# Where VectorE sums the last pair's products: ahead of the next pair's first product, or behind the plain second operand's products

## The chip, the cores and the metric

The kernel runs on one core of one Trainium2 chip. The metric is the device time of one launch in microseconds (us), taken as the median of several runs. The engines are named as in the profile: PE (TensorE, the matmuls), PEld (its weight loads), DVE (VectorE), ACT (ScalarE), POOL (GpSimd) and SP (SyncE, which only issues DMAs here). L526 is line 526 of the kernel.

## The reference

A "compressed interaction network" over `r_x` of 1024 samples, 64 fields and an embedding of 16, in float32. Cut to what matters:

```
x0 = h = x                                   # (1024, 64, 16)
for i in range(3):
    z = einsum('bfe,bge->bfge', x0, h)       # products of fields, per embedding place
    y = einsum('oc,bce->boe', W[i], z.reshape(B, 64*64, 16)) + b[i]
    x_i, h = (y[:, :64], y[:, 64:]) if i < 2 else (y, y)
    xs.append(x_i)
pooled = sum(concatenate(xs, axis=1), axis=2)   # over the embedding
return pooled @ fc_w.T + fc_b                # (1024, 1)
```

The last sum, over the 16 places of the embedding, is the one that the change moves.

## The kernel before, in words

**Tiling.** The samples are cut into 32 chunks of 32; a chunk has 32 x 16 = 512 columns. Two chunks make a pair, and there are 16 pairs. Three pairs are done in a prologue of their own form; the other thirteen (`pairs`, with `k` = 3 to 15) go through one scheme, one pair in a window of PE work.

**The work of a pair.** For each of its two chunks, called `a` and `b`, DVE multiplies field rows with rotated field rows, a block of 128 x 2048 at a time (`w_product`, recorded at L634, or `plain`/`product`, recorded at L242). A pair's blocks are named by their part in the scheme: `X` and `B21` from chunk `a`, `B22` and `T3` from chunk `b`, each with a half j = 0 and a half j = 1. `T3` is made from the sum of two operands (`w_both`, L640). POOL makes sums and differences of blocks (`w_mix`, L651; one of them is a DMA that adds, L649): `T2 = X - T3`, then `T3 = B22 + T2`, then `T2 = T2 + B21`. PE contracts the blocks with weights (`w_job`, through `mm`, L526) into the PSUM banks `alpha`, `delta` and `beta`. DVE reads those banks when a pair ends and forms products of 64 x 512 and 128 x 512 in the tile `uu` (`w_hb` L672, `w_qa` L676, `w_uu` L682, `w_ha` L679, `x_v0x` L290). Last, `sums` (L294) adds `uu` over the embedding into the pair's own columns of the tile `acc`, which nothing reads before the end of the kernel (`add_parts`, `pools`).

**PE's two columns.** The matmuls of a window come in two lists, `columns`, which `zipped` interleaves one by one; each uses its own half of PE's columns, so two run side by side. One list begins with the `X` products into `alpha`, the other with the `T3` products into `delta`. `X` goes in the order j = 1, then j = 0. So the first block that a window needs, as its very first step, is `X` with j = 1: the "first product" of this document. Which list comes first in the interleaving alternates from pair to pair. Near a window's end stand four short matmuls, `squares`, with 64 rows.

**The order of the work.** It is written out by hand. Every operation is put on a list with a planned time (`at(when, ...)`); the list is sorted by it, and the functions are called in that order, which fixes each engine's own queue. The planned times act through the order alone. Window n begins at `t = T0 + SPAN * n` with `SPAN = 31`. In it the pair `p` runs on PE, the pair before it, `q`, is ended on DVE, and the products of the next pair are made:

```
make_pair(
    t, p, (-21.4, -18.7, -18.4, -15.8, -12.2, -9.5, -6.1, -2, 1.6, 4.2),
    (-5, 1.6, 3.6, 7.2, 12.4, 18.6, 18.5),
)
quads = 30.2 if n == NPAIR - 1 else 22.9
window(t, p, (first_fill(q), second_fill(q)), late_run(q), quads=quads)
end_pair(t, q, (0.7, 11.7, 17.9, 22.3, 23.2, 18.4, 27.5))
```

The first list of `make_pair` are the times of `B22` j=0, `w_both`, `T3` j=0, `X` j=0, `B22` j=1, `w_both`, `T3` j=1, `X` j=1, `B21` j=0, `B21` j=1. The list of `end_pair` are the times of `w_hb`, `w_qa`, `w_uu`, `w_ha`, `w_uu`, `x_v0x` and `sums`, in the order of its parameters `hb_, qa, uub, ha, uua, xv, add`:

```
def end_pair(t, p, whens):
    hb_, qa, uub, ha, uua, xv, add = whens
    ...
    at(t + add, sums, p["k"])
```

A second operand is first copied into PSUM by ACT (`second`, L554), into one of two banks that rotate. Blocks come from a list of 14 (`take`, `used`). Loads are issued by SP: `xa` (L146), `xb` (L160), `e` (L164), `xx` (L169).

DVE's queue through one window, in the order before, is thus:

| place | operation | recorded at |
|---|---|---|
| 1 | `sums` of the pair before last | L294 |
| 2 | `X` j=1 of the next pair (first product) | L634 |
| 3 | `w_hb` of the pair that just ran | L672 |
| 4, 5 | `B21` j=0 and j=1 of the next pair (the plain second operand's products) | L634 |
| 6 | `B22` j=0 of the pair after it | L634 |
| 7 | `w_qa` | L676 |
| 8 to 10 | `w_both`, `T3` j=0, `X` j=0 | L640, L634 |
| 11, 12 | `w_uu` from `alpha`, `x_v0x` | L682, L290 |
| 13 to 16 | `B22` j=1, `w_both`, `w_ha`, `w_uu` from `delta` | L634, L640, L679, L682 |
| 17 | `T3` j=1; then place 1 again | L634 |

Of the kernel before, what the change touches and what calls it, by code (L numbers as in the profile page):

```python
# [70 lines left out]
def cin_kernel(ctx, tc, xra, xrb, wh, w0r, w1h, w2t, wx1, wx0, vec, out):  # L71
# [444 lines left out]
    def at(when, fn, *args, **flags):  # L516
        ops.append((when, len(ops), fn, args, flags))
# [168 lines left out]
    def make_pair(t, p, when, mixed):  # L686
        a, b = p["a"], p["b"]
        for when, c, j, name, uses in (
            (when[0], b, 2, "B22", 5), (when[1], b, 0, None, 0), (when[2], b, 0, "T3", 9),
            (when[3], a, 0, "X", 5), (when[4], b, 3, "B22", 5), (when[5], b, 1, None, 0),  # L690
            (when[6], b, 1, "T3", 9), (when[7], a, 1, "X", 13 if p["k"] > 3 else 5), (when[8], a, 2, "B21", 5),
            (when[9], a, 3, "B21", 5),
        ):
            if name is None:
                at(t + when, w_both, p, j)
                continue
            if name == "B21" and j == 2 and p["k"] == 3:
                at(t + when, w_product, p, c, j, name, uses, engine=nc.gpsimd)
                continue
            if name != "T3":  # L700
                ahead = 3.3 if p["k"] > 4 and name == "B22" and j == 2 else 2.7
                if p["k"] == 3 and name == "X" and j == 1:
                    ahead = 9.1
                at(t + when - ahead, second, c, j)
            at(t + when, w_product, p, c, j, name, uses)
        t2, t1, t4 = ("T2", "X", "T3"), ("T3", "B22", "T2"), ("T2", "T2", "B21")
        for when, j, names in zip(
            mixed, (0, 1, 1, 0, 1, 1, 0), (t2, (*t2, 0, 2), (*t2, 2), t1, t1, t4, t4)
        ):
            at(t + when, w_mix, p, j, *names)  # L710
        at(t + 29, lambda: used(p["B21"][1]))
# [4 lines left out]
    def first_fill(p):  # L716
        return [(lambda: q_extra(p["a"], va, p["beta"]),)] + p4_run(p)[-LATE : -LATE // 2]

    def second_fill(p):
        return p4_run(p)[-LATE // 2 :]  # L720

    def late_run(p, out=alpha, first=0, last=2 * NI):
        jobs = w_run(p, out, s4, "B22", out is gamma)[first:last]
        return jobs if last < 2 * NI else jobs + [(lambda: q_extra(p["b"], vb, p["alpha"]),)]
# [8 lines left out]
    def window(t, p, fill, late, pad=[], order=GROUPS[NI:] + GROUPS[:NI], quads=22.9):  # L733
        columns = (
            w_run(p, alpha, wq_all, "X", True, order=order) + fill[0] + w_run(p, alpha, s2, "T2")
            + fill[1] + w_run(p, alpha, s1, "T3"),
            w_run(p, delta, s3, "T3", True) + late + w_run(p, beta, wq_all, "B21", True, 2 * NI)
            + pad + p4_run(p)[:-LATE],
        )
        zipped(t, *columns[:: -1 if p["k"] % 2 else 1])  # L740
        at(t + quads, squares, p)
        at(t + 7.6, snap_p1, p)
        at(t + 7.8, snap_p7, p)
        at(t + 7.6 + len(fill[0]) + 8, snap_u2, p)

    def end_pair(t, p, whens):
        hb_, qa, uub, ha, uua, xv, add = whens
        at(t + hb_, w_hb, p)
        at(t + qa, w_qa, p)
        at(t + uub, w_uu, p, alpha, "A", snaps[2])  # L750
        at(t + ha, w_ha, p)
        at(t + uua, w_uu, p, delta, "O", snaps[0])
        at(t + xv, x_v0x, p["k"])
        at(t + add, sums, p["k"])


    def load_pair(t, p, b0, a0, b1, a1):
        a, b = p["a"], p["b"]
        at(t + b0, load_xa, b)
        at(t + b0, load_xb, b, 2, 0)  # L760
        at(t + a0, load_xa, a)
        at(t + a0, load_xb, a, 0)
        at(t + b1, load_xb, b, 3, 1)
        at(t + a1, load_xb, a, 1, 2, 3)
        for c in (b, a):
            at(t + 1, load_e, c)
            at(t + 14, square, c)
        at(t + 1.1, load_xx, p["k"])
# [65 lines left out]
    for n in range(NPAIR):  # L834
        k = n + 3
        s = k % 2
        p = {
            "k": k, "A": halves[s], "O": halves[1 - s], "b": 2 * k + s, "a": 2 * k + 1 - s,
        }
        pairs.append(p)  # L840
        t = T0 + SPAN * n
        if n == 0:
            load_pair(t, p, -39.9, -33.3, -33.15, -27)
            make_pair(
                t, p, (-23.4, -20.7, -20.4, -17.8, -17.2, -16.8, -16.6, -7, -13.5, 3),
                (-14, -6.9, -6.8, 7.2, 12.4, 17.6, 17.5),
            )
            left5 = [[(contract_half, 5, 3, i, n) for i in (2, 3)] for n in range(2)]
            window(
                t, p, ([left5[1][0], (q_extra, 4, va)], [left5[1][1]]),  # L850
                [left5[0][0], (q_extra, 5, va), None, None], [left5[0][1], None],
                GROUPS, 21.9,
            )
        else:
            q = pairs[-2]
            load_pair(t, p, -34, -28, -27.8, -27.7)
# [3 lines that stand above are left out]
            )  # L860
            quads = 30.2 if n == NPAIR - 1 else 22.9
            window(t, p, (first_fill(q), second_fill(q)), late_run(q), quads=quads)
            end_pair(t, q, (0.7, 11.7, 17.9, 22.3, 23.2, 18.4, 27.5))


    NP = NCH // 2
# [37 lines left out]
    t, q = T0 + SPAN * NPAIR, pairs[-1]  # L904
# [183 lines left out]
```

## Time and profile before

| | |
|---|---|
| median of 3 runs | 452.44 us (451.9 to 452.5) |
| profiled execution | 453.01 us, of which the span of the trace is 451.2 us |
| PE | busy 445.1 us, 99% of the span |
| DVE | busy 393.1 us, 87% |
| POOL | busy 364.4 us, 81% |
| ACT | busy 116.8 us, 26% |
| granted clock of PE | 1.00 |
| `sums` in its full form, 128 x 1024 to 128 x 64 | 13 times, 1.209 us each |

The span is the time from the first to the last instruction of the program; the device time has 1.8 us more around it. Busy time of PE is modelled, since matmuls overlap, so that a busy PE may still lose time between two starts. Where such losses lie is read from the starts in the timeline.

### The profile page before, as it was taken

The page shows a single profiled execution, that of the slowest core. Times are in us where ns is not written, and L with a number is a line of the kernel's source. Part 1 is how long each engine was busy: PE and PEld are TensorE (multiplying, and loading weights), DVE is VectorE, ACT ScalarE, POOL GpSimd, SP SyncE. Part 2 cuts the span into 40 slices and gives each one's busy share as a digit, 9 for nine tenths or more (in the row PEclk, how much of TensorE's full clock was granted, in tenths as well). Part 3 has the DMA queues.
Part 4 walks back from the last instruction along what each step waited for, and adds up shares of the span by engine and source line. Part 5 has one row for each costly group of instructions (what it writes and reads, how often), then busy time and mean ns, then how long its engine had stood idle before and what let it go on. Part 6 is the DMA issues. An engine that isn't in the chain of part 4 may idle for free.

```text
span 451.2 us, 6067 instructions
## 1 busy us (share of the span) xinstructions
PE 445.1 (99%) x2302; PEld 178.9 (40%) x2302; DVE 393.1 (87%) x284; ACT 116.8 (26%) x215; POOL 364.4 (81%) x125
## 2 busy tenths in 40 slices
PE   7999999999999999999999999999999999999997
PEld 4565343442334433343333433344333433344435
DVE  3996598998989998999999899999989999998734
ACT  2163241323312213231221313131131313114111
POOL 5413687999996979899797979979797997979900
PEclk9999999999999999999999999999999999999999
DMA  8996999395949386694958769493967949591500
GB/s 297 415 306 157 322 393 359 114 336 155 324 114 333 121 226 256 133 360 105 281 179 230 259 153 336 107 319 135 252 238 161 341 105 314 176 270 44 107 0 2
DMA packets 34484, 99.67 MB, mean 221 GB/s; under 512 B 6324, under 2 KB 6996, under 8 KB 27864
## 3 DMA queue, kind: packets, MB, share of 16 engines
q1 hardware_dynamic: 31800, 84.70, 52.5%
q0 software_dynamic: 1872, 13.63, 16.9%
q10 hardware_dynamic: 784, 0.95, 0.8%
q8 instruction: 18, 0.29, 0.3%
q14 instruction: 10, 0.08, 0.0%
HBM read 84.00 MB, written 1.64 MB: 190 GB/s over the span
## 4 chain that ended last, share of the span: by engine, by line
PE 96%; DMA 2%; POOL 1%; SPq 0%; issue 0%; DVE 0%; ACT 0%; POOLq 0%; ACTq 0%
PE alpha L526 45%; PE delta L526 20%; PE beta L526 10%; PE acc L526 6%; PE acc L252 6%; PE q L526 3%; PE acc L270 3%; DMA z<-in_w0r 2%; POOL z L651 1%; PE y L526 0%; PE pm L386 0%; PE pv L359 0%; SPq L146 0%; PE xp L221 0%; PE hx L526 0%
## 5 line engine op out<-in xcount | busy, mean ns | idle before, releaser
L651 POOL TENSOR_TENSOR z<-z,z 128x2048 f32<-128x2048 f32 (+1 forms) x78 | 299.6, 3874 | 29.2 <-PE alpha L526 29.1
L634 DVE TENSOR_TENSOR z<-xa,xp 128x2048 f32<-128x2048 f32 x103 | 231.7, 2279 | 2.6 <-issue 1.4
L526 PE MATMUL alpha<-z,ws 128*64 128x512 f32 x624 | 222.1, 593 | 0.0
L526 PEld LDWEIGHTS alpha<-z,ws 128*64 128x64 f32 x624 | 71.7, 137 | 86.3 <-issue 85.5
L526 PE MATMUL delta<-z,w_all 128*64 128x512 f32 x208 | 95.6, 593 | 0.7 <-POOL z L651 0.7
L554 ACT COPY xp<-xb 128x512 f32<-128x512 f32 x88 | 51.6, 588 | 169.5 <-DVE z L634 141.6
L526 PE MATMUL beta<-z,w_all 128*64 128x512 f32 x208 | 93.8, 595 | 0.0
L526 PE MATMUL alpha<-z,w_all 128*64 128x512 f32 x208 | 92.0, 595 | 0.0
L526 PE MATMUL delta<-z,ws 128*64 128x512 f32 x208 | 91.6, 593 | 0.0
L242 DVE TENSOR_TENSOR z<-xa,xp 128x2048 f32<-128x2048 f32 (+2 forms) x23 | 45.0, 2002 | 6.3 <-ACT xp L554 4.8
L242 POOL TENSOR_TENSOR z<-xa,xb 128x2048 f32<-128x2048 f32 x6 | 27.5, 4646 | 19.6 <-DMA xb<-in_xrb 19.6
L526 PEld LDWEIGHTS delta<-z,w_all 128*64 128x64 f32 x208 | 28.3, 137 | 32.9 <-issue 30.4
L526 PEld LDWEIGHTS alpha<-z,w_all 128*64 128x64 f32 x208 | 27.5, 137 | 29.9 <-issue 24.0
L526 PEld LDWEIGHTS delta<-z,ws 128*64 128x64 f32 x208 | 28.1, 137 | 23.7 <-issue 22.8
L526 PEld LDWEIGHTS beta<-z,w_all 128*64 128x64 f32 x208 | 26.9, 137 | 24.2 <-issue 23.0
L252 PE MATMUL acc<-z,w_all 128*64 128x256 f32 x256 | 29.1, 382 | 2.3 <-DVE z L242 2.0
L526 PE MATMUL acc<-z,w_all 128*64 128x512 f32 (+1 forms) x96 | 29.7, 594 | 0.0
L252 PEld LDWEIGHTS acc<-z,w_all 128*64 128x64 f32 x256 | 18.0, 137 | 14.6 <-DVE z L242 3.8
L665 ACT ACTIVATE snap<-alpha,vs 64x512 f32<-64x512 f32 x13 | 8.9, 684 | 54.8 <-PE alpha L526 54.8
L294 DVE TENSOR_REDUCE acc<-uu 128x64 f32<-128x1024 f32 (+2 forms) x19 | 19.6, 1036 | 0.2
L682 DVE SCALAR_TENSOR_TENSOR uu<-alpha,snap 64x512 f32<-64x512 f32 x13 | 9.0, 689 | 12.2 <-PE alpha L526 12.2
L662 ACT COPY snap<-alpha 64x512 f32<-64x512 f32 x13 | 7.6, 581 | 46.2 <-PE alpha L526 29.7
(117 smaller groups left out, 356.4 us busy)
## 6 DMA issues: line engine op xcount, KB each, us to landing
xa<-in_xra SPq DMA_DIRECT2D x32, 1024.0 KB, 8.5
xb<-in_xrb SPq DMA_DIRECT2D x128, 256.0 KB, 8.0
z<-z POOLq DMA_DIRECT2D x13, 1024.0 KB, 8.5
e<-in_xra SPq DMA_DIRECT2D x28, 128.0 KB, 7.3
xx<-in_xra SPq DMA_DIRECT2D x28, 128.0 KB, 2.5
z<-in_w2t SPq DMA_DIRECT2D x2, 1024.0 KB
z<-in_wx SPq DMA_DIRECT2D x2, 1024.0 KB, 10.0
z<-in_w1h SPq DMA_DIRECT2D x1, 1024.0 KB
```

The lines of the kernel that those rows point to most:

```text
L242: engine.tensor_tensor(blocks[zs[c, j]][:, at, :], xas[c][:, at, :], xbs[c][j].unsqueeze(1).to_broadcast([128, last - first, N]), ALU.mult,)
L252: nc.tensor.matmul(accs[c][halves[n]], w_all[:, t, 0:64], blocks[zs[c, j]][:, i, n * H2 : (n + 1) * H2], start=(t == 0), stop=(j == last a ...
L270: nc.tensor.matmul(accs[c][halves[1 - c % 2]], w_all[:, t, 64:128], blocks[zs[c, j]][:, i, :], start=(t == 0), stop=False, skip_group_chec ...
L294: nc.vector.tensor_reduce(acc[rows, of, k, half], uu[rows, of if at is None else at, E * half.start : E * half.stop].rearrange("p k (b e) ...
L526: nc.tensor.matmul(out, w, rhs, start=start, stop=stop, skip_group_check=True)
L554: nc.scalar.copy(bank, xbs[c][j])
L634: engine.tensor_tensor(blocks[b], xas[c], xbs[c][j].unsqueeze(1).to_broadcast([128, NI, N]), ALU.mult)
L651: nc.gpsimd.tensor_tensor(*(blocks[b][:, first:last] for b in (o, x, y)), ALU.subtract if in1 == "T3" else ALU.add,)
L662: nc.scalar.copy(snaps[0][p["O"]], alpha(p))
L665: nc.scalar.activation(snaps[1][p["O"]], alpha(p), AF.Identity, bias=bh1[p["A"]])
L682: nc.vector.scalar_tensor_tensor(uu[p[out], 0], x(p), 1.0 / QS, factor[p[out]], ALU.mult, ALU.mult)
```

## The change

The sum's planned time in `end_pair` goes from 27.5 to 36, for the twelve pairs that this call ends:

```diff
-            end_pair(t, q, (0.7, 11.7, 17.9, 22.3, 23.2, 18.4, 27.5))
+            end_pair(t, q, (0.7, 11.7, 17.9, 22.3, 23.2, 18.4, 36))
```

In window n the next pair's `X` j=1 stands at t + 31 - 2 = t + 29, `w_hb` of the running pair at t + 31.7, `B21` at t + 32.6 and t + 35.2, and the following `B22` j=0 at t + 40.6. So `sums` moves from place 1 of the table to behind place 5: the order becomes `X` j=1, `w_hb`, `B21`, `B21`, `sums`, `B22`. For the last of the twelve, in the kernel's tail, it moves from behind the last plain product to behind `w_hb`. The queues of PE, ACT, POOL and SP hold the same instructions in the same order, and no instruction is added or taken away.

## The prediction

> **What bounds the kernel now.** I read the page first, then PE's list of waits, then the timelines of PE and DVE round a window's start. The page says that PE is the bound and that DVE is not far behind:
>
> ```profile
> PE 445.1 (99%) x2302; PEld 178.9 (40%) x2302; DVE 393.1 (87%) x284; ACT 116.8 (26%) x215; POOL 364.4 (81%) x125
> ```
>
> PE's waits over the whole run show only the prologue (the last one, for POOL, ends at 107.17 us). From 125 us on that list is empty:
>
> ```profile
> PE acc L252 <- DVE z L242: 2.0, 1, 2.0
> PE misc L115 <- PEq L1077: 0.8, 1, 0.8
> PE delta L526 <- POOL z L651: 0.7, 1, 0.7
> PE acc L252 <- DVE w_all L302: 0.2, 1, 0.2
> ```
>
> But busy time is modelled, so I looked at starts. PE's timeline where the window at 216 us begins (columns: start, duration, instruction):
>
> ```profile
> 215.41 0.59 PE L526 MATMUL delta<-z,w_all 128*64 128x512 f32 x1
> 215.42 0.59 PE L526 MATMUL alpha<-z,ws 128*64 128x512 f32 x1
> 215.84 0.59 PE L526 MATMUL delta<-z,w_all 128*64 128x512 f32 x1
> 215.85 0.59 PE L526 MATMUL alpha<-z,ws 128*64 128x512 f32 x1
> 216.38 0.64 PE L526 MATMUL alpha<-z,w_all 128*64 128x512 f32 x1
> 216.39 0.64 PE L526 MATMUL delta<-z,ws 128*64 128x512 f32 x1
> 216.86 0.59 PE L526 MATMUL alpha<-z,w_all 128*64 128x512 f32 x1
> 217.29 0.59 PE L526 MATMUL alpha<-z,w_all 128*64 128x512 f32 x1
> ```
>
> Starts in a column are 0.43 apart, but here come steps of 0.54 and 0.48: 0.16 us is lost, and the first matmul is recorded at 0.64 in place of 0.59. Now DVE over the same stretch and up to its next meeting with PE:
>
> ```profile
> 212.92 1.21 DVE L294 TENSOR_REDUCE acc<-uu 128x64 f32<-128x1024 f32 x1
> 214.06 2.27 DVE L634 TENSOR_TENSOR z<-xa,xp 128x2048 f32<-128x2048 f32 x1
> 216.49 0.76 DVE L672 SCALAR_TENSOR_TENSOR snap<-alpha,vs,snap 64x512 f32<-64x512 f32 x1 [0.16 <-PE alpha L526]
> 217.28 6.68 DVE L634 TENSOR_TENSOR z<-xa,xp 128x2048 f32<-128x2048 f32 x3
> 224.36 0.68 DVE L676 TENSOR_TENSOR snap<-beta,snap 64x512 f32<-64x512 f32 x1 [0.40 <-PE beta L526]
> 225.07 0.70 DVE L640 TENSOR_TENSOR xp<-xp,xb 128x512 f32<-128x512 f32 x1
> 225.81 4.49 DVE L634 TENSOR_TENSOR z<-xa,xp 128x2048 f32<-128x2048 f32 x2
> 231.24 0.69 DVE L682 SCALAR_TENSOR_TENSOR uu<-alpha,snap 64x512 f32<-64x512 f32 x1 [0.95 <-PE alpha L526]
> ```
>
> The first product ends at 214.06 + 2.27 = 216.33, and PE's first `alpha<-z,w_all` of the window starts at 216.38, 0.05 later. The same 0.05 to 0.06 stands between the two at every start from 137.8 to 399.5 us, eleven times. Once the product was early: it ended at 108.08 + 2.29 = 110.37 and its matmul started at 110.65, 0.43 after the one ahead of it at 110.22, with nothing lost. So the lost time is a wait for the first product, too short for the list of waits. The sum, 1.21 us, stands straight ahead of that product.
>
> **What the Trainium skill says.** "TensorE: Matmul & The Clock Gate", Part 3, The mechanism: matmuls start and end strictly in program order; only weight loads are pulled ahead. So a matmul held for its block holds what follows, in both columns. The trace agrees: at 216.38 `delta` was held too, though its block was ready. In windows whose list has `delta` first, `delta` started on time (190.15) and only `alpha` came late (190.17, next 190.65). The same page, Single matmul latency: an isolated matmul also pays for its drain, which a stream hides; the trace agrees with 0.64 against 0.59 and the step of 0.48. "Perfetto Trace Analysis", Identifying the Most-Contended Engine: matmul busy share is no measure of headroom; here 99% busy goes with 0.16 us lost in a window. "SBUF — State Buffer", Who interferes with whom: POOL's port contends with DVE instructions of two SBUF inputs, and `tensor_reduce` takes no 2-port mode. The moved sum reads `uu` alone, so moving it beside other POOL work should not stretch it; its 13 full forms last 1.209 us on average, with POOL busy beside most.
>
> **The change part by part.**
>
> *Out of the way of the first product: 11 times.* The change moves twelve sums; eleven stand ahead of a window's first product (the windows at 137.8 to 399.5), the twelfth stands in the tail. Start to start the sum takes 214.06 - 212.92 = 1.14 us. So the first product may start at 212.92 and end at 215.2, some 1.1 us ahead of its need. Nothing else holds it: its operand was copied to PSUM by ACT at 207.44, long before; its block was last read by PE at about 208.4. In the windows of the other parity POOL reads the block last (the addition ending at 236.68), and the product would start at 239.06.
>
> The gain is not 1.14 us a window: PE has only the wait to get back. In the five windows that start with `alpha` (164.04, 216.38, 268.73, 321.07, 373.41) both columns lose 0.54 + 0.48 - 2 x 0.43 = 0.16 us. In the six that start with `delta` (137.8, 190.2, 242.5, 294.9, 347.2, 399.5) only the second column loses, and the loss is paid at the next `squares`, which follow after a step of 0.59 instead of 0.53 (209.47 to 210.05 against 235.75 to 236.28): 0.06 us. The sum is 5 x 0.16 + 6 x 0.06 = 1.16 us. A check: from `squares` to `squares` the stretches of the two kinds are 26.21 to 26.23 and 26.11 to 26.12 us; less 0.16 and 0.06 both come to 26.06. An upper bound is PE with no wait: 60 steps of 0.4285 and 0.31 us round `squares` (steps of 0.53, 0.48, 0.54 and 0.48) make 26.02, against a mean of 26.17: 0.15 x 11 = 1.6 us.
>
> *Where the sum lands.* `w_hb` waits for PE's `alpha`, so the time saved ahead of it turns into idle time of DVE: about 0.16 + 1.14 = 1.3 us. `B21` and `B21` run as now. Then the sum delays `B22` j=0 by 1.14 us. `w_qa` now idles 0.40 waiting for `beta`; that absorbs part, and `w_qa`, `w_both`, `T3` j=0 and `X` j=0 come 0.75 to 0.85 us later. `X` j=0 ends at 225.81 + 4.49 = 230.30 and would end at about 231.1. The next wait is `w_uu` for `alpha`, released at 231.24: it absorbs the rest, with about 0.1 us to spare. PE's earlier window start takes up to 0.05 of that; if `w_uu` is 0.1 late, the first product is still 1.0 us early. So I price the landing at nothing; the covers are two waits for PE (0.40 and 0.95).
>
> *Who waits for the delayed ones.* `X` j=0 and `T3` j=0 go to POOL's subtraction, which starts at 237.19 after other work of POOL (6.9 us to spare), and to PE at 242.5 or later. `B22` j=0 is read by POOL some 25 us later. The end of `T3` j=0 frees the bank for ACT's copy at 228.13; that copy comes 0.8 later, and its product starts at 232.62. `w_qa` frees `beta`, which PE takes again about 6 us later. No load waits for the sum or the delayed ones in this stretch: SP's loads follow `T3` j=1 (213.04) and the second `B21` (221.79), which keep their times. `acc` is read only at the end.
>
> *Tail.* The twelfth sum (423.75) moves behind `w_hb` (425.68, idle 0.72 before it) and ahead of `w_qa` at 432.08, before which DVE idles 5.64 us: nothing.
>
> Sum: 1.16 us less, 1.2 in round numbers. The profiled execution would go from 453.01 to about 451.8 and its span from 451.2 to 450.0. The profiled execution lies 0.57 above the median, so I take the difference from the median: 452.44 - 1.2 = 451.2 us.
>
> **The rivals.**
>
> *The time is not given back, or half of it.* PE may meet another wait inside those 0.16 us, or the loss at a window's start may be partly a cost of the switch of banks. Against it: the start at 110.65 lost nothing, and the next closest block (POOL's last `T2` sum, 236.68) is 2.4 us early. For it: no wait of this size is named anywhere. If only one kind of window gains, it is 0.4 to 0.8 us: 451.6 to 452.0, and to 452.6 with the readings' scatter.
>
> *The delayed stretch becomes the bound (slower).* DVE from `w_hb`'s release at 216.49 to `w_uu`'s at 231.24 has 14.75 us, and the new order fills about 14.6. Whatever exceeds it pushes `w_uu` and all behind it. It decides once the excess passes the 1.1 us that the first product has won; then each window pays the rest. With an excess of 1.3 us that is 0.2 x 11 = 2.2 us: 454.6. Against it: it needs the sum and the four delayed operations to take 1.3 us more in their new place, where no new data or port use comes in.
>
> *It does nothing.* Were the sum to stay ahead of the first product, nothing would change; planned times 29 and 36 exclude that.
>
> **How the numbers follow.** About 0.2% (0.9 us) is what a measurement of this kernel can tell from no change. The first case (0.8 to 1.6 us less) has 0.78, the half gain 0.17, the slower one 0.05. The first case's estimate of 1.2 lies only 0.3 above the bound, so of its 0.78 I give 0.07 to "same"; of the half gain 0.01 is left to faster and 0.01 to slower. Faster 0.72, same 0.22, slower 0.06. The range starts at 452.44 - 1.6 less 0.2 of scatter, 450.6, and ends at a gain of about 0.2, 452.2.
>
> **What would show it right or wrong.** Right: PE's starts at the eleven window starts 0.43 apart, the first product ending about 1.1 us ahead of its matmul; DVE idle about 1.3 us before L672, close to nothing before L676, and at most 0.2 before L682 from `alpha`; `squares` to `squares` 26.06 in both kinds of window. Wrong: steps of 0.54 that remain with the product early, a new wait of PE, or the first product again 0.05 ahead of its matmul.

## The result and the profile after

The changed kernel takes 451.29 us (median of 22 runs, 450.27 to 453.16) against 452.41 us (median of 22 runs beside them, 451.5 to 454.18). The ratio is 0.9972, 95% interval 0.9962 to 0.9983: 1.27 us less by the ratio, with 0.8 to 1.7 us as its interval. It is faster, and by about the 1.2 us of the forecast.

The profiled execution of the changed kernel is the slowest of its 22 (453.16 us, span 451.4 us), so the spans of the two pages don't show the gain. The page's first part:

```profile
PE 443.7 (98%) x2302; PEld 160.2 (35%) x2302; DVE 392.4 (87%) x284; ACT 116.8 (26%) x215; POOL 364.6 (81%) x125
```

PE's waits from 100 us on name two. Both end before 121 us, ahead of the first of the moved sums, where the change touches nothing:

```profile
PE delta L526 <- POOL z L651: 1.1, 1, 1.1
PE delta L526 <- DMA z<-z: 0.8, 1, 0.8
```

The execution of before had lost 0.7 us there. So the two traces are compared from a fixed point behind it: the `squares` of the window n = 1. They start at 131.59 us before and at 132.90 after, 1.31 later. From there to the `squares` of the last window it is 424.57 - 131.59 = 292.98 us before and 424.73 - 132.90 = 291.83 after: 1.15 us less. From those to the end both take 26.6 us. 451.2 + 1.31 - 1.15 = 451.4, the span of after.

PE's timeline at the start of the window that answers to the one at 216 us (start, duration, instruction):

```profile
216.88 0.59 PE L526 MATMUL delta<-z,w_all 128*64 128x512 f32 x1
216.89 0.59 PE L526 MATMUL alpha<-z,ws 128*64 128x512 f32 x1
217.31 0.59 PE L526 MATMUL alpha<-z,w_all 128*64 128x512 f32 x1
217.31 0.59 PE L526 MATMUL delta<-z,ws 128*64 128x512 f32 x1
217.74 0.59 PE L526 MATMUL alpha<-z,w_all 128*64 128x512 f32 x1
```

The steps of 0.54 and 0.48 are gone: 0.43 throughout, and no matmul of 0.64. VectorE's timeline of the same stretch (in brackets the idle time before an instruction and what ended it):

```profile
211.81 4.49 DVE L634 TENSOR_TENSOR z<-xa,xp 128x2048 f32<-128x2048 f32 x2
217.53 0.76 DVE L672 SCALAR_TENSOR_TENSOR snap<-alpha,vs,snap 64x512 f32<-64x512 f32 x1 [1.23 <-PE alpha L526]
218.31 4.48 DVE L634 TENSOR_TENSOR z<-xa,xp 128x2048 f32<-128x2048 f32 x2
222.72 1.22 DVE L294 TENSOR_REDUCE acc<-uu 128x64 f32<-128x1024 f32 x1
...
226.04 0.68 DVE L676 TENSOR_TENSOR snap<-beta,snap 64x512 f32<-64x512 f32 x1
...
227.48 4.48 DVE L634 TENSOR_TENSOR z<-xa,xp 128x2048 f32<-128x2048 f32 x2
232.12 0.69 DVE L682 SCALAR_TENSOR_TENSOR uu<-alpha,snap 64x512 f32<-64x512 f32 x1 [0.15 <-PE alpha L526]
```

The first product is the second of the two at 211.81. It ends at 216.30, 1.01 us ahead of its matmul at 217.31. `w_hb` (L672) idles 1.23 us, `w_qa` (L676) no longer idles, `w_uu` (L682) still idles 0.15. The moved sums last 1.20 to 1.22 us in their new place, as in the old one. The stretches from `squares` to `squares`, two of before and then the two of after (length; busy time of PE, PEld, DVE, ACT and POOL; granted clock; share and GB/s of DMA):

```profile
183.93:210.05 26.12, 26.12 (x126) 11.03 (x124) 24.40 (x18) 6.37 (x11) 23.64 (x8) 1.00 0.75 222
210.05:236.28 26.23, 26.23 (x127) 8.37 (x125) 24.51 (x18) 6.32 (x11) 23.62 (x8) 1.00 0.75 221
```

```profile
185.03:211.09 26.06, 26.06 (x127) 8.45 (x125) 24.34 (x18) 6.37 (x11) 23.62 (x8) 1.00 0.76 223
211.09:237.15 26.06, 26.06 (x126) 8.45 (x125) 24.46 (x18) 6.32 (x11) 23.63 (x8) 1.00 0.75 222
```

All ten stretches of after between the `squares` of n = 1 and n = 11 are 26.06 or 26.07 us long.

### The profile page after: what moved, and what is told of

It is laid out like the page before. It is cut to its first block, busy times and chain, and to the rows that moved or that the text cites. A ratio compares the mean times of both kernels' runs of the same rounds, so it can differ in the third digit from the quotient of the medians.

```text
span 451.4 us, 6067 instructions
## 1 busy us (share of the span) xinstructions
PE 443.7 (98%) x2302; PEld 160.2 (35%) x2302; DVE 392.4 (87%) x284; ACT 116.8 (26%) x215; POOL 364.6 (81%) x125
## 4 chain that ended last, share of the span: by engine, by line
PE 76%; DMA 12%; DVE 5%; SPq 3%; POOL 2%; issue 1%; ACT 1%; DVEq 0%; POOLq 0%
PE alpha L526 39%; PE delta L526 19%; PE beta L526 10%; DMA xb<-in_xrb 6%; PE q L526 3%; DVE z L634 3%; DMA z<-z 3%; PE acc L252 2%; DMA xa<-in_xra 1%; DMA md<-z 1%; POOL z L242 1%; SPq L459 1%; POOL z L537 1%; SPq L419 0%; ACT z L400 0%
## 5 line engine op out<-in xcount | busy, mean ns | idle before, releaser
L634 DVE TENSOR_TENSOR z<-xa,xp 128x2048 f32<-128x2048 f32 x103 | 231.6, 2279 | 2.4 <-issue 1.2
L526 PE MATMUL alpha<-z,ws 128*64 128x512 f32 x624 | 221.8, 593 | 0.0
L526 PEld LDWEIGHTS alpha<-z,ws 128*64 128x64 f32 x624 | 68.2, 137 | 91.7 <-issue 91.4
L526 PE MATMUL delta<-z,w_all 128*64 128x512 f32 x208 | 95.6, 593 | 1.9 <-POOL z L651 1.1
L526 PE MATMUL beta<-z,w_all 128*64 128x512 f32 x208 | 93.8, 595 | 0.0
L526 PE MATMUL alpha<-z,w_all 128*64 128x512 f32 x208 | 91.4, 592 | 0.0
L526 PE MATMUL delta<-z,ws 128*64 128x512 f32 x208 | 91.4, 592 | 0.0
L242 POOL TENSOR_TENSOR z<-xa,xb 128x2048 f32<-128x2048 f32 x6 | 27.5, 4634 | 19.7 <-DMA xb<-in_xrb 19.7
L526 PEld LDWEIGHTS delta<-z,w_all 128*64 128x64 f32 x208 | 28.3, 137 | 34.5 <-issue 30.8
L526 PEld LDWEIGHTS alpha<-z,w_all 128*64 128x64 f32 x208 | 28.4, 137 | 31.7 <-issue 31.2
L526 PEld LDWEIGHTS delta<-z,ws 128*64 128x64 f32 x208 | 28.5, 137 | 27.7 <-issue 27.4
L526 PEld LDWEIGHTS beta<-z,w_all 128*64 128x64 f32 x208 | 26.9, 137 | 28.6 <-issue 28.3
L526 PE MATMUL acc<-z,w_all 128*64 128x512 f32 (+1 forms) x96 | 29.4, 594 | 0.0
L672 DVE SCALAR_TENSOR_TENSOR snap<-alpha,vs,snap 64x512 f32<-64x512 f32 x13 | 9.8, 750 | 17.9 <-PE alpha L526 9.6
```

Of the source, the lines that this page charges most:

```text
L242: engine.tensor_tensor(blocks[zs[c, j]][:, at, :], xas[c][:, at, :], xbs[c][j].unsqueeze(1).to_broadcast([128, last - first, N]), ALU.mult,)
L526: nc.tensor.matmul(out, w, rhs, start=start, stop=stop, skip_group_check=True)
L634: engine.tensor_tensor(blocks[b], xas[c], xbs[c][j].unsqueeze(1).to_broadcast([128, NI, N]), ALU.mult)
L672: nc.vector.scalar_tensor_tensor(hb_, alpha(p), bh1[p["A"]], hb_, ALU.add, ALU.add)
```

## The experiments

The theory: VectorE's work from the release of `w_uu` (the end of the last matmul into `alpha` that it waits for) to the first product is a chain that PE waits for at each window's start; the sum was one link of it, and with the link gone PE runs without a wait, at 26.06 us a window. The rivals are these: the place behind `B21` has a cost of its own; the cost came of the sum and the product standing side by side; the lost time is PE's own at a switch of banks; the delayed stretch binds. Times of eight kernels follow, each with its ratio to the kernel before run on the same chip.

**Another place out of the chain: `beside_hb`.** The sum stands between the first product and `w_hb`.

```diff
-            end_pair(t, q, (0.7, 11.7, 17.9, 22.3, 23.2, 18.4, 27.5))
+            end_pair(t, q, (0.7, 11.7, 17.9, 22.3, 23.2, 18.4, 29.5))
```

> The sum stands between the first product and w_hb (planned time 29.5), where the changed kernel leaves VectorE idle for about 1.2 us. Chain theory (the sum costs only because it stands in VectorE's chain from w_uu's release to the first product): as the changed kernel, about 451.3 us, squares to squares 26.06 us in all windows, idle before w_hb about 0.1 us, before w_qa 0.4, before w_uu from alpha 0.9. Rival, the place behind the B21 products has a cost of its own: then this kernel is faster than the changed one, 450.5 us or less. Rival, the lost time has nothing to do with the sum's being ahead of the first product: 452.4.

Measured: 450.92 us (12 runs), ratio 0.9973 (0.9959 to 0.9987), as the changed kernel's 0.9972. VectorE's timeline:

```profile
209.46 4.49 DVE L634 TENSOR_TENSOR z<-xa,xp 128x2048 f32<-128x2048 f32 x2
213.86 1.21 DVE L294 TENSOR_REDUCE acc<-uu 128x64 f32<-128x1024 f32 x1
215.17 0.76 DVE L672 SCALAR_TENSOR_TENSOR snap<-alpha,vs,snap 64x512 f32<-64x512 f32 x1
...
222.88 0.68 DVE L676 TENSOR_TENSOR snap<-beta,snap 64x512 f32<-64x512 f32 x1 [0.23 <-PE beta L526]
...
229.76 0.69 DVE L682 SCALAR_TENSOR_TENSOR uu<-alpha,snap 64x512 f32<-64x512 f32 x1 [0.95 <-PE alpha L526]
```

The sum fills time in which VectorE would wait for PE before `w_hb`; all stretches are again 26.06 us, and `w_uu` keeps an idle time of 0.95. So the landing behind `B21` costs nothing that this place would save, and 26.06 is again what PE takes when the product is in time.

**Earlier, but still in the chain: `ahead_of_t3`.**

```diff
-            end_pair(t, q, (0.7, 11.7, 17.9, 22.3, 23.2, 18.4, 27.5))
+            end_pair(t, q, (0.7, 11.7, 17.9, 22.3, 23.2, 18.4, 23.5))
```

> The sum goes one product earlier, ahead of T3 j=1 (planned time 23.5), so it no longer stands next to the first product but is still in the chain before it. Chain theory: no change from before, about 452.4 us, the first product again 0.05 us ahead of its matmul, squares to squares 26.2 and 26.1. Rival, the cost comes of the two standing side by side (the sum waits for the w_uu just ahead of it, the product for the sum): about 451.3, as the changed kernel.

Measured: 453.48 us (17 runs), ratio 1.0021 (1.0012 to 1.0031): about 1 us slower than before, where no change was expected. The product again ends 0.05 ahead of its matmul, so the chain still binds; standing side by side is not the cause. The chain has become longer:

```profile
210.54 0.69 DVE L682 SCALAR_TENSOR_TENSOR uu<-delta,snap 64x512 f32<-64x512 f32 x1
211.27 1.22 DVE L294 TENSOR_REDUCE acc<-uu 128x64 f32<-128x1024 f32 x1
212.50 4.49 DVE L634 TENSOR_TENSOR z<-xa,xp 128x2048 f32<-128x2048 f32 x2
```

The `T3` product now starts 1.23 us after the sum's start, where the first product before started 1.14 after it. From `w_uu`'s start to the first product's end it is 212.50 + 4.49 - 210.54 = 6.45 us; before it was 214.06 + 2.27 - 209.99 = 6.34. In the windows that begin with `delta` the same 0.1 us comes ahead of the sum. The sum now reads the `uu` that the `w_uu` just ahead of it writes; whether that is what costs the 0.1 us is not shown.

From the `squares` of n = 1 to the last it is 293.66 us, 0.68 more than before: 0.06 a window, about half of what the chain grew. Where `delta` is first, the stretch is 26.25 instead of 26.12 us. There `alpha`'s column now starts 0.14 us behind `delta`'s (0.01 before), and `w_uu`, released from `delta`'s column, comes 14.65 us after the first product's matmul instead of 14.78. These 0.13 us pay for the growth at the next start, and that stretch stays at 26.21. The expectation had left out both the growth and this lead.

**The dose, in the old place: `two_ahead`.**

```diff
         at(t + add, sums, p["k"])
+        if add == 27.5:
+            at(t + add, sums, p["k"])
```

> The kernel before with each of the twelve sums done twice in its old place (the second repeats the first). Chain theory: the first product comes 1.14 us later in eleven windows and PE waits for it, 11 x 1.14 = 12.5 us more, about 465 us, squares to squares 27.3. Rival, VectorE has slack there and the loss at a window's start is PE's own: at most 1 us more, 453.4 or less.

Measured: 463.1 us (4 runs), ratio 1.0232 (1.021 to 1.0254): 10.5 us more, not 12.5; between the `squares` of n = 1 and the last it is 9.93 us more. PE's wait for the product is now named, `PE alpha L526 <- DVE z L634`, eleven times. PE at two successive window starts, the first with `delta` first, the second with `alpha` first:

```profile
192.17 0.59 PE L526 MATMUL alpha<-z,ws 128*64 128x512 f32 x1
...
192.60 1.02 PE L526 MATMUL delta<-z,ws 128*64 128x512 f32 x2
193.87 0.64 PE L526 MATMUL alpha<-z,w_all 128*64 128x512 f32 x1 [0.25 <-DVE z L634]
193.88 0.64 PE L526 MATMUL delta<-z,ws 128*64 128x512 f32 x1
...
219.55 0.59 PE L526 MATMUL delta<-z,w_all 128*64 128x512 f32 x1
219.55 0.59 PE L526 MATMUL alpha<-z,ws 128*64 128x512 f32 x1
220.57 0.64 PE L526 MATMUL alpha<-z,w_all 128*64 128x512 f32 x1 [0.42 <-DVE z L634]
220.57 0.64 PE L526 MATMUL delta<-z,ws 128*64 128x512 f32 x1
```

Where `delta` is first, its matmul (two records of the trace, 1.02 us together) runs while `alpha` waits. `delta`'s column is then ahead, and the matmuls whose end releases `w_uu` run in that column: `w_uu` comes 14.00 us after the first product's matmul, where it came 14.78 us after it before. So the windows that begin with `delta` give 0.78 us of the dose back, at the next start. The dose itself is a little larger than the 1.14 us of the expectation:

```profile
215.85 2.47 DVE L294 TENSOR_REDUCE acc<-uu 128x64 f32<-128x1024 f32 x2
218.23 2.28 DVE L634 TENSOR_TENSOR z<-xa,xp 128x2048 f32<-128x2048 f32 x1
```

From the start of the two sums to the start of the product it is 218.23 - 215.85 = 2.38 us, where the one sum took 1.13 to 1.14 before: 1.25 us more. Two windows pay twice 1.25 less 0.78, which is 1.72 us. The stretches are 27.38 and 26.70 us, 54.08 together against 52.34 before: 1.74 more. The mechanism holds; one link of its price, how a column's lead is handed on, was missing in the expectation.

**The dose, in the new place: `two_behind` and `three_behind`.** The changed kernel with the sum repeated once (the diff) and twice (the same line two times):

```diff
         at(t + add, sums, p["k"])
+        if add == 36:
+            at(t + add, sums, p["k"])
```

> The changed kernel with each of the twelve sums done twice in its new place (the second repeats the first). Chain theory with the spare time that the prediction gave the first product (1.1 us): w_uu from alpha comes about 1.0 us late, the first product ends 0.1 us or less ahead of its need, the time is between that of the changed kernel and that of before, 451.3 to 452.4. Rival, the delayed stretch has no spare time and all that passes w_uu's release is paid: 1.0 x 11 = 11 us more, about 462.

Measured: 451.81 us (20 runs), ratio 0.9985 (0.9974 to 0.9995), within the expected stretch. `w_uu` no longer waits for PE. From n = 3 on, the first window whose product comes behind a doubled sum, the product is 0.13 ahead where `delta` is first. Where `alpha` is first it is 0.05 ahead, and PE loses 0.1 us again:

```profile
157.09:183.25 26.16, 26.16 (x127) 8.37 (x125) 25.62 (x19) 6.32 (x11) 23.70 (x8) 1.00 0.73 221
183.25:209.31 26.06, 26.06 (x127) 8.51 (x125) 25.54 (x19) 6.37 (x11) 23.63 (x8) 1.00 0.75 223
```

> The changed kernel with each of the twelve sums done three times in its new place (repeats). Chain theory: 2 x 1.14 = 2.3 us more in the stretch, of which 0.15 is absorbed before w_uu from alpha and 1.1 by the spare time of the first product; the rest, about 1.0 to 1.1 us, is paid in each of eleven windows: 11 to 12 us more than the changed kernel, 462 to 463.5. Rival, no spare time at the first product: 2.1 x 11 = 23 us more, 474. Rival, VectorE does not bind at all: 451.3.

Measured: 461.78 us (4 runs), ratio 1.0211 (1.0192 to 1.0229): 9.6 us more than before and 10.8 more than the changed kernel by the two ratios; between the two `squares` it is 10.40 more than the changed kernel. The 1.0 us for each window is as expected, but ten windows pay it, not eleven: the sums stand behind the start of the windows n = 2 to 12 and in the tail, so the first product that they delay is that of n = 3. The first stretch, up to the `squares` of n = 2, is 26.06 us, and from n = 3 on the stretches settle at 27.09 and 27.04. VectorE runs from `w_uu` (L682) to `w_hb` (L672) and round again with no wait for PE in either kind of window:

```profile
210.07 0.68 DVE L682 SCALAR_TENSOR_TENSOR uu<-alpha,snap 64x512 f32<-64x512 f32 x1
...
215.83 4.49 DVE L634 TENSOR_TENSOR z<-xa,xp 128x2048 f32<-128x2048 f32 x2
220.35 0.76 DVE L672 SCALAR_TENSOR_TENSOR snap<-alpha,vs,snap 64x512 f32<-64x512 f32 x1
```

So the new place has room for one more sum, almost exactly, and a third makes VectorE the bound.

**One kind of window at a time: `alpha_windows` and `delta_windows`.** The sum is moved only ahead of the windows that begin with `alpha`, or only ahead of those that begin with `delta`:

```diff
-            end_pair(t, q, (0.7, 11.7, 17.9, 22.3, 23.2, 18.4, 27.5))
+            end_pair(t, q, (0.7, 11.7, 17.9, 22.3, 23.2, 18.4, 27.5 if n % 2 or n == NPAIR - 1 else 36))
```

```diff
-            end_pair(t, q, (0.7, 11.7, 17.9, 22.3, 23.2, 18.4, 27.5))
+            end_pair(t, q, (0.7, 11.7, 17.9, 22.3, 23.2, 18.4, 36 if n % 2 else 27.5))
```

> The sum is moved only ahead of the five windows whose matmuls begin with alpha. Prediction's sizes: 5 x 0.16 = 0.8 us less than before, about 451.6 us; the stretches from squares to squares with such a window come to 26.06, the others stay at 26.12. Rival, each of the eleven windows pays the same 0.1 us: 0.5 us less, 451.9, both kinds of stretch between.

> The sum is moved only ahead of the six windows whose matmuls begin with delta. Prediction's sizes: 6 x 0.06 = 0.36 us less than before, about 452.05 us; the stretches with such a window come to 26.06, the others stay at 26.22. Rival, each of the eleven windows pays the same 0.1 us: 0.6 us less, 451.8.

Measured: `alpha_windows` 452.02 us, ratio 0.9985 (0.9974 to 0.9996); `delta_windows` 452.43 us, ratio 0.9994 (0.9982 to 1.0006), 14 runs each. In both fences the upper stretch holds a window start with `delta` first, the lower one a start with `alpha` first. Of `alpha_windows`:

```profile
183.93:210.05 26.12, 26.12 (x126) 11.14 (x124) 24.41 (x18) 6.37 (x11) 23.63 (x8) 1.00 0.73 222
210.05:236.11 26.06, 26.06 (x126) 8.45 (x124) 24.40 (x18) 6.32 (x11) 23.63 (x8) 1.00 0.74 222
```

Of `delta_windows`:

```profile
183.22:209.28 26.06, 26.06 (x127) 8.45 (x125) 24.34 (x18) 6.37 (x11) 23.56 (x8) 1.00 0.73 223
209.28:235.56 26.28, 26.28 (x126) 8.36 (x124) 24.56 (x18) 6.32 (x11) 23.68 (x8) 1.00 0.76 220
```

`alpha_windows` does as expected: from the `squares` of n = 1 to the last it is 292.19 us, 0.79 less than before. `delta_windows` does not: it is 292.92, only 0.06 less, where 0.36 were expected. The moved windows fall to 26.06, but the others rise from 26.22 to 26.28, and only the last start, which no further one follows, keeps its 0.06. From `delta`'s first matmul of one window to `alpha`'s of the next it is 215.67 - 189.44 = 26.23 us, and 216.38 - 190.15 = 26.23 before: the chain runs from `delta`'s column through `w_uu` to the next product, and the late `alpha` column stood outside of it. What is won at one start is lost at the next. The timed intervals of these two kernels, 0.2% wide, can't tell this; the traces do.

**Another operation in the sum's old place: `other_op_ahead`.** To the changed kernel this is added:

```diff
         at(t + add, sums, p["k"])
+        if add == 36:
+            at(t + 28.5, w_uu, p, delta, "O", snaps[0])
```

> The changed kernel with another operation of VectorE in the sum's old place: w_uu from delta, 64 x 512, 0.69 us, is repeated ahead of the first product. Chain theory: the first product has 1.1 us to spare, so it ends 0.4 us ahead of its need and nothing is lost: about 451.3 us, squares to squares 26.06. Rival, any operation between T3 j=1 and the first product costs PE its wait, whatever the spare time: 452.4.

Measured: 451.28 us (19 runs), ratio 0.9972 (0.9961 to 0.9983). The product ends 0.57 ahead of its matmul where `delta` is first and 0.16 where `alpha` is first (the two lines below: 214.04 + 2.29 = 216.33 against 216.49); all stretches are 26.06.

```profile
214.04 2.29 DVE L634 TENSOR_TENSOR z<-xa,xp 128x2048 f32<-128x2048 f32 x1
216.49 0.59 PE L526 MATMUL alpha<-z,w_all 128*64 128x512 f32 x1
```

What stands ahead of the product costs nothing as long as the product is in time.

## Why the prediction was right

- **The wait under the busy share.** The step that carried it was the 0.05 us from the product's end to its matmul, together with the one start where the product was early and nothing was lost. The steps of 0.54 and 0.48 vanished in the changed kernel, and steps of 0.47 and 0.48 came back with `two_behind`, in the windows where the product was late again. The rival of a cost of PE's own at the switch of banks falls.
- **The gain's size.** Forecast 1.16 us; the traces show 1.15 between the same two `squares`, the timed ratio 1.27 (0.8 to 1.7). The floor was forecast at 26.06 us a window; it is 26.06, in three kernels. The upper bound of 1.6 us rested on a floor of 26.02, too low by 0.04.
- **The split of the gain** into 5 x 0.16 and 6 x 0.06 is the term that doesn't hold as it was put. The 0.16 is right: alone the five return 0.79. The 0.06 of a window that begins with `delta` is not a loss of its own unless the next start is in time too; alone the six return 0.06 in all, at the last window. The sum of both is right because the change moves both; for `delta_windows` the same prices gave 0.36, six times too much.
- **The landing.** `w_hb` idles 1.23 and 1.37 (forecast 1.3), `w_qa` at most 0.03, `w_uu` 0.15 (forecast "about 0.1 us to spare"), the product is 1.01 and 1.17 ahead (forecast 1.1).
- **The slower rival** was placed rightly: it decides from an excess of 1.1 us. One repeated sum (1.14 us) brings the product back to its matmul and costs 0.5 us between the two `squares`; two cost about 10 us. Its count of eleven windows was one too many: the moved sums delay ten first products. With the change alone the excess is nil.

## What to carry to other kernels

A busy share of 99% can hide a wait that recurs in every iteration: compare the steps between starts at an iteration's edge with the usual step, and look for a product that ends the same short time ahead of its use each time. Then ask which operations between the last meeting of the two engines and that product needn't be there; an operation that nobody reads soon belongs where its engine waits anyway. The gain is bounded by the consumer's lost steps, here 0.1 us a window, not by the length of what was moved, 1.14 us.

## What the runs showed of the hardware that was not expected

- Two matmul streams in the two halves of PE's columns can be out of step. Where `alpha`'s first matmul was held, `delta`'s earlier one ran on, and the lead was kept until the `squares`. In the kernel before it was 0.06 us (190.58 and 190.65, still 209.47 and 209.53), and both columns began the `squares` at 210.05 and 210.06. In `two_ahead` it was a whole matmul, and gave back 0.78 us of a later wait.
- PEld's busy time went with such a lead. It was 11.0 us in the stretches of before whose `alpha` column was some 0.06 late and 14.36 in those of `ahead_of_t3`, where it was 0.19 late. It was 8.4 to 8.6 where the columns started together or a whole matmul apart. The number of loads is the same, and the stretch need not be longer by as much. Over the whole run it fell from 178.9 to 160.2 us with the change. Why it follows the lead is not shown.
- From the `squares` of n = 1 to the last it is 291.83 us in each of three kernels (the changed one, `beside_hb`, `other_op_ahead`), though their profiled executions span 451.4, 449.0 and 450.6 us. What differs lies ahead of that point, which comes at 132.90, 130.55 and 132.09 us.
